# Two layers of state-space mixing and routed experts: the second layer's output with tokens on partitions, its mean from centred matrices, D x seeded by ScalarE, the gate by tanh

## The chip, the core and the metric

The kernel runs on one core of a Trainium2 chip. A core has TensorE (PE; its weight loads are listed as PEld), VectorE (DVE), ScalarE (ACT), GpSimd (POOL) and SyncE (SP, which here only issues DMAs), a memory SBUF and an accumulator memory PSUM, both of 128 partitions. Each engine executes its own queue in order; semaphores tie the queues together. The metric is the device time of one execution in microseconds, the lower the better.

## What is computed

Everything is fp32. The input x is (4, 256, 64, 64), that is 16384 tokens of 256 channels. The reference, cut to what the change touches:

```python
# layer 0, per batch; tokens = x as (L = 4096, 256), times w_in.T
z   = sigmoid(silu(tokens @ w_gate.T + b_gate))
t   = layernorm(tokens)
...                                   # Mamba scan with D_INNER = 512, 16 states
y   = ys + Dp * xm                    # xm: the convolved, Silu'd input of the scan
y   = (y * silu(zm)) @ out_w.T
x1  = tokens + (y * z) @ w_out.T + x  # the residual of layer 0

# layer 1, on t = x1 as tokens
u   = layernorm(t)                    # eps 1e-5
xn  = rmsnorm(u)
...                                   # SSD with 8 heads of 64, 64 states
y   = rmsnorm(y * silu(z), 1e-5)
t   = t + (u + y @ W_out.T)
logits = layernorm(t) @ gate_w + gate_b          # 8 experts, the best one is taken
t   = t + prob * expert(layernorm(t))            # capacity 2560 tokens per expert
```

## The kernel before

Three stages follow each other: `mixers` (both mixing layers and the routing, to about 6035 us of the profiled execution), `experts` (to about 7360 us) and `turn` (the transposition of the result). The change lies in `mixers`, but for the place of some columns in a row that the experts read.

`mixers` works on 64 chunks of T = 256 tokens (16 in each of 4 batches). Channels lie on partitions, tokens along the free dimension. For a chunk the parts are recorded by functions: `front0` (projections, norm and convolution of layer 0), `mid0` (gate, dt, B and C), `scan` (the recurrence, in 16 units of 1024 columns: ACT makes the decays `da`, DVE multiplies `ub` and scans `h`, POOL multiplies `p` with C, PE sums over states into `py`), `tail0` (output of layer 0 and the residual x1), `front1` (norms, projections and convolution of layer 1), `ssd` (two blocks of 128 tokens, s = 0 and 1) and `back1` (output of layer 1, routing).

Nothing is issued while it is recorded. `Plan` keeps every operation with its reads, its writes, an assumed duration (the `weight`s in `mm`, `act`, `dve`, `gps`) and a slot: chunk number times 16 plus the number in `at(...)`. `Plan.order` is a list scheduler over the five queues: at each moment an engine takes, among the operations that could start, the one with the smallest slot. A tile with `bufs` buffers is begun only when one is free, and DVE operations that read two SBUF tensors are kept apart from POOL's. The result is a fixed order on each engine. So a change of one operation or of one weight can move all the others. `silus` keeps the Silus of one point together, between two loads of ACT's tables.

What the change touches, with the names and lines of before:

- `D x`: `scan` puts `diag_d0[:, j]` times `gx` into `py` by a matmul (line 846), before the 16 sums of that j. `py` has one buffer for two j. DVE multiplies it with the gate's half of `gx` into `g`, 256 columns for each j (line 859).
- The gate: `mid0` makes sigmoid of the Silu by Exp, Ln and Exp on ACT (lines 738, 743, 744) and stores it as `z_d`; `tail0` loads it and multiplies (line 874).
- x1 and its norm: `tail0` copies x1 from PSUM (line 883); `front1` makes its mean with the constant matrix `mean_c` (line 892), subtracts it on DVE (`xc`, line 894), squares, averages, makes two reciprocal roots (one for xn, one for u) and the residual `res` = u + x1 by two DVE operations (lines 911, 912).
- The state of `ssd`: decay times state, and the addition of the new part (lines 1064, 1065), each 256 columns, twice a chunk.
- `back1`: the mean of squares over 512 channels by `mean_c` (line 1078), `W_out` as the stationary operand with 256 tokens moving (line 1084), `t2` = product x root + `res` by two DVE operations (lines 1086, 1087), then the transposition of `t2` to tokens on partitions (line 1094), the routing scores as a further product (line 1098), a copy into `row` (line 1103), from which the tokens go out, and the statistics for the experts' norm.

The setup, ahead of `r = Plan(tc)`, is written directly and stands first in every queue.

Of the kernel before, what the change touches and what calls it, by code (L numbers as in the profile page):

```python
# [20 lines left out]
P = 128  # L21
# [24 lines left out]
ROW = C + 4  # L46
# [86 lines left out]
class Plan:  # L133
# [67 lines left out]
    def mm(self, out, left, right, **kw):  # L201
        rows, n = out.shape[0], self.width(right)
        w = max(0.3, n / 600) if rows > 64 else max(0.2, n / 1000) if rows > 32 else max(0.2, n / 1100)
        self.note("PE", w, self.nc.tensor.matmul, (out, left, right), kw, (out,), (left, right), join=out.root)
# [162 lines left out]
def tile_conv_attn_hybrid(ctx: ExitStack, tc: tile.TileContext, a: dict, out: bass.AP, cap: int, st: int):  # L367
# [36 lines left out]
    def mixers(es):  # L404
# [45 lines left out]
        s_out = load("W_out", nc.scalar)  # L450
# [7 lines left out]
        for k in range(KD):  # L458
            ts(s_out[:, k], s_out[:, k], s_gn[:, k : k + 1], None, ALU.mult)
# [17 lines left out]
        before = mask("before", -1, -1, 1)  # L477
# [10 lines left out]
        diag_d0 = diagonal(m_d, "diag_d0")  # L488
# [52 lines left out]

        m_inb = wp.tile([P, 2 * KD], F32, name="m_inb", tag="m_inb")
# [16 lines left out]

        rank = wp.tile([P, NE], F32, name="rank", tag="rank")  # L560
# [11 lines left out]
        nc.gpsimd.memset(blank[:, C + 3 :], float(NT))  # L572
# [35 lines left out]
        def silus(*tiles):  # L608

            calls = [(nc.scalar.activation, (t, t, AF.Silu), t, t) for t in tiles]  # L610
            calls.append((nc.scalar.preload_act_table_set, (SETS,), None, None))
# [50 lines left out]
        class Chunk:  # L662
            def __init__(self, i, b, c):
                self.i, self.b, self.c = i, b, c

            def at(self, n):

                r.slot(self.i * NST, n)
# [55 lines left out]
        def mid0(k_):  # L724
# [5 lines left out]
            r.dma("ACT", k_.gx_d.rearrange("k p l -> p k l"), pre0[:, KC:])  # L730
            k_.at(MID0 + 1)
# [4 lines left out]

            z = pre0[:, :KC]
            r.act(z, z, AF.Exp, scale=-1.0)
# [4 lines left out]
            r.act(z, z, AF.Ln, bias=one_c)  # L743
            r.act(z, z, AF.Exp, scale=-1.0)
            k_.z_d = scratch([KC, P, T], "z_d")
            r.dma("ACT", k_.z_d.rearrange("k p l -> p k l"), z)
# [41 lines left out]
        def scan(k_):  # L788
# [11 lines left out]
            for j in range(KD):  # L800
# [10 lines left out]
                dt4, u4 = both  # L811

                gx = work([P, 2, T], "gx", 2)
                r.dma("SP", gx, k_.gx_d.rearrange("(s j) p l -> j p s l", s=2)[j])
                sl = slice(j * SQ, (j + 1) * SQ)
                if later:

                    k_.at(j * SQ - 1)
# [4 lines left out]
                for f in range(SQ):  # L823
# [19 lines left out]
                    if f == 0:  # L843
                        if j % 2 == 0:
                            py = bank_y(2, T)
                        r.mm(py[:, j % 2], diag_d0[:, j], gx[:, 1], start=True, stop=False, skip_group_check=True)
                    for i in range(SQ):
# [5 lines left out]
                            stop=f == SQ - 1 and i == SQ - 1,  # L853
# [5 lines left out]
                r.tt(k_.g[:, j], gx[:, 0], py[:, j % 2], ALU.mult)  # L859
# [3 lines left out]
        def tail0(k_):  # L863
# [10 lines left out]
            r.tt(z, z, po, ALU.mult)  # L874
# [7 lines left out]
            k_.x1 = x1 = z  # L882
            r.copy(x1, po)

        def front1(k_):

            first = k_.c == 0
            x1 = k_.x1
            k_.at(TAIL + 2)
            pm = bank_b(T)  # L890
            for k in range(KC):
                r.mm(pm, mean_c, x1[:, k], start=k == 0, stop=k == KC - 1)
            xc = work([P, KC, T], "xc1")
            r.tt(xc, x1, pm[:, None, :].to_broadcast([P, KC, T]), ALU.subtract)
# [3 lines left out]
            pv = bank_b(T)  # L898
            for k in range(KC):
                r.mm(pv, mean_c, sq[:, k], start=k == 0, stop=k == KC - 1)  # L900

            rboth = work([P, T], "rstd", 2)
            rstd = work([P, T], "rstd", 2)
            r.act(rboth, pv, AF.Ln, bias=epsb_c, scale=1.0 + EPS)
            r.act(rstd, pv, AF.Ln, bias=eps5_c)
            r.act(rboth, rboth, AF.Exp, scale=-0.5)
            r.act(rstd, rstd, AF.Exp, scale=-0.5)
            xn = work([P, KC, T], "t")
            r.tt(xn, xc, over_channels(rboth), ALU.mult)
            k_.res = res = work([P, KC, T], "res1", 2)  # L910
            r.tt(res, xc, over_channels(rstd), ALU.mult)
            r.tt(res, res, x1, ALU.add)
# [476 lines left out]
```

## Time and profile before

| | us |
|---|---|
| median of 3 runs | 7476.55 |
| lowest and highest of them | 7471.62, 7479.49 |
| the profiled execution | 7447.88 |
| its span, first to last instruction | 7446.1 |
| busy in it: PE, DVE | 6483.4, 5935.5 |
| busy in it: ACT, POOL | 4791.0, 3129.4 |
| mean granted TensorE clock | 0.938 of full speed |

The rows below and the prediction come from the profiled execution. A group of instructions is given by its line in the source, its engine, its operation, the tile written and the tiles read (buffer numbers left out), the shapes and the count; then the busy time, the mean duration of one, and the idle time of the engine just before these instructions, with what ended it. Nearly all operations of `mixers` have the line 356, where the plan issues them, so they are told apart by their tiles. An fp32 matmul stands as two MATMUL and two LDWEIGHTS records. Busy time counts overlapping records once; a mean counts each in full.

### The profile page before, as it was taken

The numbers are of one execution on the slowest core, as the hardware profiler recorded it, in microseconds if no ns is written. First come the engines' busy times: TensorE is split into PE (matmuls) and PEld (weight loads), VectorE is DVE, ScalarE is ACT, GpSimd is POOL, SyncE is SP. The second block draws the span as 40 slices with busy tenths as digits, with TensorE's granted clock in tenths as the row PEclk, the third lists the DMA queues.
The fourth block names the chain that finished last, engine by engine and source line by source line (L and its number), as shares of the span: only waits on it lengthen the run. The fifth ranks groups of instructions, "written<-read, shape, count | busy, mean of one in ns | idle before, by whom it ended". The sixth has DMA issues, their size and how long they took to land. (4 is left out here: it accounts for less than half of the span.)

```text
span 7446.1 us, 114562 instructions
## 1 busy us (share of the span) xinstructions
PE 6483.4 (87%) x38320; PEld 4211.9 (57%) x38320; DVE 5935.5 (80%) x7459; ACT 4791.0 (64%) x11351; POOL 3129.4 (42%) x2436
## 2 busy tenths in 40 slices
PE   4788888888888888888988888888888879999996
PEld 3555555555555555555555555555555556666664
DVE  4799999999999999999999999999999823333332
ACT  4677787777777788777877777777777621111111
POOL 3455455454455455555554555554555401111110
PEclk7899999999999999999999999999999889999998
DMA  7766666666666666666666666666666321111115
GB/s 196 206 171 170 170 172 166 170 170 168 172 169 170 169 169 167 173 174 172 175 172 170 169 170 172 171 170 170 168 174 170 101 63 43 50 45 37 44 32 185
DMA packets 1157215, 1106.25 MB, mean 149 GB/s; under 512 B 127512, under 2 KB 1137316, under 8 KB 1156370
## 3 DMA queue, kind: packets, MB, share of 16 engines
q1 hardware_dynamic: 967362, 884.52, 46.9%
q10 hardware_dynamic: 175440, 180.83, 7.4%
q0 software_dynamic: 13824, 33.58, 1.3%
q8 instruction: 305, 5.00, 0.3%
q14 instruction: 284, 2.33, 0.1%
HBM read 780.64 MB, written 313.85 MB: 147 GB/s over the span
## 5 line engine op out<-in xcount | busy, mean ns | idle before, releaser
L356 POOL TENSOR_TENSOR p<-h,bc 128x1024 f32<-128x1024 f32 x1024 | 2414.9, 2359 | 2133.6 <-DVE ub L356 1221.2
L356 DVE TENSOR_TENSOR_SCAN h<-da,ub 128x1024 f32<-128x1024 f32 x1024 | 2339.7, 2285 | 108.0 <-ACT da L356 6.2
L356 ACT ACTIVATE da<-dt,w_m_Alog 128x255 f32<-128x255 f32 x4096 | 1807.4, 498 | 94.3 <-DMA dt<-dt_d 80.7
L356 DVE TENSOR_TENSOR ub<-u,bc 128x1024 f32<-128x1024 f32 x1024 | 1367.7, 1336 | 34.3 <-DMA u<-u_d 13.9
L356 PE MATMUL py<-p,sum 128*32 128x256 f32 x8192 | 704.4, 420 | 194.4 <-POOL p L356 192.2
L1246 ACT ACTIVATE hid<-ph,b 128x512 f32<-128x512 f32 x160 | 109.2, 682 | 1029.7 <-PE ph L1244 871.4
L1266 POOL DMA_INDIRECT tok_d<-fixed,number x160 | 156.9, 981 | 1164.8 <-DVE fixed L1264 833.0
L356 PE MATMUL b<-t,w_W_in 128*128 128x256 f32 x2304 | 594.9, 401 | 27.7 <-DVE dv L356 18.1
L1255 PE MATMUL po<-w,hid 128*128 128x256 f32 x2560 | 591.2, 384 | 5.1 <-DVE y L1257 5.0
L1244 PE MATMUL ph<-xt,w 128*128 128x512 f32 x1280 | 561.7, 597 | 14.1 <-DVE xt L1239 14.1
L1255 PEld LDWEIGHTS po<-w,hid 128*128 128x128 f32 x2560 | 476.7, 190 | 122.3 <-issue 55.6
L356 PEld LDWEIGHTS b<-t,w_W_in 128*128 128x128 f32 x2304 | 429.0, 195 | 150.4 <-DVE dv L356 45.9
L356 PEld LDWEIGHTS py<-p,sum 128*32 128x32 f32 x8192 | 200.7, 114 | 537.3 <-POOL p L356 314.2
L356 PE MATMUL a<-t,w_m_in_w 128*128 128x256 f32 x2048 | 479.9, 388 | 10.9 <-DVE t L356 10.7
L356 PEld LDWEIGHTS a<-t,w_m_in_w 128*128 128x128 f32 x2048 | 381.3, 191 | 113.1 <-DVE t L356 26.0
L356 ACT COPY hlast<-h 128x4 f32<-128x4 f32 x1024 | 197.0, 196 | 381.5 <-DVE h L356 358.5
L1244 PEld LDWEIGHTS ph<-xt,w 128*128 128x128 f32 x1280 | 240.6, 190 | 311.8 <-issue 287.5
L1257 DVE TENSOR_SCALAR y<-po,rows 128x256 f32<-128x256 f32 x160 | 76.4, 481 | 380.0 <-PE po L1256 380.0
L356 ACT ACTIVATE pre<-pre 128x512 f32<-128x512 f32 (+2 forms) x256 | 352.5, 1377 | 12.8 <-ACT dbl L356 9.7
L356 PE MATMUL c<-cum,after 128*128 128x512 f32 x512 | 330.0, 762 | 32.5 <-DVE state L356 27.9
L356 PE MATMUL b<-raw,taps_x 128*32 128x256 f32 x2048 | 175.0, 414 | 206.4 <-DMA raw<-raw_d 150.2
L356 ACT ACTIVATE cum<-upto,da 128x128 f32<-128x128 f32 x1024 | 333.9, 391 | 4.8 <-DVE da L356 4.5
(224 smaller groups left out, 11461.6 us busy)
## 6 DMA issues: line engine op xcount, KB each, us to landing
raw<-raw_d SPq DMA_DIRECT2D x2048, 128.0 KB
dt<-dt_d SPq DMA_DIRECT2D x1024, 128.0 KB
u<-u_d SPq DMA_DIRECT2D x1024, 128.0 KB
raw_d<-raw ACTq DMA_DIRECT2D x128, 518.0 KB
gx_d<-pre ACTq DMA_DIRECT2D x64, 1024.0 KB
gx<-gx_d SPq DMA_DIRECT2D x256, 256.0 KB
bc<-bc_d SPq DMA_DIRECT2D x2048, 32.0 KB
dt_d<-mid SPq DMA_DIRECT2D x64, 512.0 KB
```

Source lines behind the costliest of these rows:

```text
L356: op.issued = f(*map(placed, args), **{k: placed(v) for k, v in kw.items()})
L1244: mm(ph, w1[:, k, f * P : (f + 1) * P], xt[:, k], start=k == 0, stop=k == KC - 1)
L1246: act(hid[:, f], ph, AF.Relu, bias=b1[:, f : f + 1])
L1255: mm(po, hid[:, f, j * P : (j + 1) * P], w2[:, f], start=f == 0, stop=False)
L1257: ts(y[:, j], po, rows[:, j, C : C + 1], None, ALU.mult)
L1266: nc.gpsimd.indirect_dma_start(out=tok_d, out_offset=bass.IndirectOffsetOnAxis(ap=number[:, j : j + 1], axis=0), in_=fixed[:, j], in_offse ...
```

## The change

- The matrices of layer 0's residual (`w_in` plus the identity) and output (`w_out`, halved) have their mean over output channels taken out in the setup, so that what `tail0` copies from PSUM is already the centred x1, `xc`. The mean itself is made only as a column per token, from the vectors `mean_res` and `mean_out`.
- `front1` makes the reciprocal root of the norm twice: as before over all partitions for xn, and as a column per token (`cols`) together with the mean. Each column comes from matmuls with the tokens as the stationary operand and one moving column. `res` is gone.
- `back1` transposes `xc` and adds the score columns in the same bank; ACT scales it with `cols` into `xr`, that is the residual u + x1 and its scores, tokens on partitions. `W_out` has eight more columns (its product with the scores' matrix, made in the setup) and is now the moving operand, the tokens the stationary one. One DVE operation per 128 tokens makes product x root + `xr` straight into `row`. The statistics and the scores read `row`.
- `D x`: ACT writes it into `py` as a scaled copy, for two j at once, ahead of the sums; `g` is made for two j, 512 columns, and `gx` loaded for two.
- The gate: sigmoid(v) is (1 + tanh(v/2))/2. The Tanh stands with the Silus, the 1 is added in the multiplication of `tail0`, the half is in `w_out`.
- The state: one scalar_tensor_tensor for each of four 64-column heads, in place of two instructions over all.
- The plan's weight of a matmul with at most 16 columns is 0.13 instead of 0.3. The four routing columns of `row` stand ahead of the 256 channels instead of behind.

```diff
     def mm(self, out, left, right, **kw):
-        w = max(0.3, n / 600) if rows > 64 else max(0.2, n / 1000) if rows > 32 else max(0.2, n / 1100)
+        w = 0.13 if n <= 16 else max(0.3, n / 600) if rows > 64 else max(0.2, n / 1000) if rows > 32 else max(0.2, n / 1100)
...
-        diag_d0 = diagonal(m_d, "diag_d0")
...
+        def centre(w, name):
+            means = wp.tile([P, KC], F32, name=name, tag=name)
+            for k in range(KC):
+                nc.vector.tensor_reduce(means[:, k : k + 1], w[:, k], AX.X, ALU.add)
+            ts(means, means, 1.0 / C, None, ALU.mult)
+            for k in range(KC):
+                ts(w[:, k], w[:, k], means[:, k : k + 1], None, ALU.subtract)
+            return means
+
+        mean_res = centre(w_res, "mean_res")
+        ts(w_out, w_out, 0.5, None, ALU.mult)
+        mean_out = centre(w_out, "mean_out")
...
+        for k in range(KD):
+            pt_s = bank_a()
+            for m in range(KC):
+                nc.tensor.transpose(pt_s[:, m * P : (m + 1) * P], s_out[:, k, m * P : (m + 1) * P], ident)
+            turned = wk.tile([P, KC, P], F32, name=nm("turned"), tag="sq", bufs=1)
+            nc.scalar.copy(turned, pt_s[:, :C].rearrange("p (m l) -> p m l", m=KC))
+            pt_s = bank_a()
+            for m in range(KC):
+                mm(pt_s[:, :NE], turned[:, m], g_cen[:, m], start=m == 0, stop=m == KC - 1)
+            nc.scalar.copy(s_out[:, k, C:], pt_s[:, :NE])
+
+        py = py_p.tile([P, 512], F32, name="py0", tag="py", bufs=1)
+        mm(py, ident, s_in[:, 0, :512], start=True, stop=True)
...
+        def half_tanh(t):
+            return nc.scalar.activation(t, t, AF.Tanh, scale=0.5)
+
-        def silus(*tiles):
+        def silus(*tiles, gates=0):
             calls = [(nc.scalar.activation, (t, t, AF.Silu), t, t) for t in tiles]
+            calls += [(half_tanh, (t[:, :KC],), t[:, :KC], t[:, :KC]) for t in tiles[:gates]]
...
-            r.act(z, z, AF.Exp, scale=-1.0)
-            r.act(z, z, AF.Ln, bias=one_c)
-            r.act(z, z, AF.Exp, scale=-1.0)
...
-                gx = work([P, 2, T], "gx", 2)
-                r.dma("SP", gx, k_.gx_d.rearrange("(s j) p l -> j p s l", s=2)[j])
+                if j % 2 == 0:
+                    gx = work([P, 2, 2, T], "gx", 2)
+                    for s in range(2):
+                        r.dma("SP", gx[:, s], k_.gx_d[s * KD + j : s * KD + j + 2].rearrange("j p l -> p j l"))
...
-                        r.mm(py[:, j % 2], diag_d0[:, j], gx[:, 1], start=True, stop=False, skip_group_check=True)
+                            for i in range(2):
+                                r.act(py[:, i], gx[:, 1, i], AF.Copy, scale=m_d[:, j + i : j + i + 1])
...
-                r.tt(k_.g[:, j], gx[:, 0], py[:, j % 2], ALU.mult)
+                if j % 2 == 1:
+                    r.tt(k_.g[:, j - 1 : j + 1], gx[:, 0], py, ALU.mult)
...
-            r.tt(z, z, po, ALU.mult)
+            r.dve("scalar_tensor_tensor", z, z, 1.0, po, ALU.add, ALU.mult)
...
-            k_.x1 = x1 = z
-            r.copy(x1, po)
+            k_.xc = work([P, KC, T], "xc", 2)
+            r.copy(k_.xc, po)
+            k_.x1 = (xin, z)
...
-            pm = bank_b(T)
-            for k in range(KC):
-                r.mm(pm, mean_c, x1[:, k], start=k == 0, stop=k == KC - 1)
-            xc = work([P, KC, T], "xc1")
-            r.tt(xc, x1, pm[:, None, :].to_broadcast([P, KC, T]), ALU.subtract)
...
+            for s in range(NS):
+                for k in range(KC):
+                    r.mm(pv[:, T + s : T + s + 1], sq[:, k, s * Q : (s + 1) * Q], mean_c[:, :1], ...)
+            for s in range(NS):
+                for i, (part, means) in enumerate(zip(k_.x1, (mean_res, mean_out))):
+                    for k in range(KC):
+                        r.mm(pv[:, T + NS + s : T + NS + s + 1], part[:, k, s * Q : (s + 1) * Q], means[:, k : k + 1], ...)
...
-            r.act(rstd, pv, AF.Ln, bias=eps5_c)
+            r.act(cols[:, :NS], pv[:, T : T + NS], AF.Ln, bias=eps5_c)
+            r.copy(cols[:, NS:], pv[:, T + NS :])
...
-            r.tt(res, xc, over_channels(rstd), ALU.mult)
-            r.tt(res, res, x1, ALU.add)
+            r.act(cols[:, :NS], cols[:, :NS], AF.Exp, scale=-0.5)
+            r.act(cols[:, :NS], cols[:, :NS], AF.Identity, bias=one_c)
...
-                r.tt(new, state, hend[:, :, None].to_broadcast([P, hh, HD]), ALU.mult)
-                r.tt(new, new, ph, ALU.add)
+                for h in range(hh):
+                    r.dve("scalar_tensor_tensor", new[:, h], state[:, h], hend[:, h : h + 1], ph[:, h], ALU.mult, ALU.add)
...
+            for s in range(NS):
+                pr = bank_c(C + NE)
+                for k in range(KC):
+                    r.transpose(pr[:, k * P : (k + 1) * P], k_.xc[:, k, toks], ident)
+                for k in range(KC):
+                    r.mm(pr[:, C:], k_.xc[:, k, toks], g_cen[:, k], start=k == 0, stop=k == KC - 1)
+                xr = work([P, C + NE], "xr", 2)
+                r.act(xr, pr, AF.Identity, scale=k_.cols[:, s : s + 1], bias=k_.cols[:, NS + s : NS + s + 1])
...
-            for k in range(KD):
-                r.mm(pm, mean_c, k_.sq[:, k], start=k == 0, stop=k == KD - 1)
+            for s in range(NS):
+                for k in range(KD):
+                    r.mm(pm[:, s : s + 1], k_.sq[:, k, s * Q : (s + 1) * Q], mean_c[:, :1], ...)
...
-            r.tt(t2, po, over_channels(rr), ALU.mult)
-            r.tt(t2, t2, k_.res, ALU.add)
+                for k in range(KD):
+                    r.mm(po, sz[:, k, s * Q : (s + 1) * Q], s_out[:, k], start=k == 0, stop=k == KD - 1)
+                r.dve("scalar_tensor_tensor", row[:, s, TOK:], po, rr[:, s : s + 1], xrs[s], ALU.mult, ALU.add)
...
-            for s in range(NS):
-                r.copy(row[:, s, :C], pr[:, s])
```

## The prediction

> **What bounds the kernel now.** I read the page's slices first, then the busy time of each engine by stage, then the groups of instructions inside a steady millisecond of the first stage, then the waits there, and last the timeline of the setup.
>
> The slices (tenths of busy time in 40 equal parts of the span) show two regimes: 32 slices in which VectorE (DVE) is at nine tenths, then eight in which TensorE (PE) is.
>
> ```profile
> PE   4788888888888888888988888888888879999996
> DVE  4799999999999999999999999999999823333332
> ACT  4677787777777788777877777777777621111111
> ```
>
> Busy time by stage, in the column order of the first line:
>
> ```profile
> core 0: us, PE busy (x) PEld busy (x) DVE busy (x) ACT busy (x) POOL busy (x), PEclk, DMA share, GB/s
> 2500.00:3500.00 1000.00, 877.28 (x5776) 573.20 (x5775) 930.68 (x1153) 789.96 (x1890) 507.38 (x380) 0.95 0.66 171
> 6100.00:7200.00 1100.00, 1083.11 (x3797) 675.64 (x3795) 415.70 (x577) 160.06 (x272) 133.36 (x136) 1.00 0.14 42
> ```
>
> The second is the experts, PE-bound, and the change leaves their arithmetic alone. The first is the stage it edits. DVE has 69 us of idle time in 1000. The groups of that millisecond (busy us, mean ns of one, then the idle time just before them):
>
> ```profile
> L356 DVE TENSOR_TENSOR_SCAN h<-da,ub 128x1024 f32<-128x1024 f32 x177 | 404.4, 2285 | 17.4 <-DVE ub L356 0.7
> ...
> L356 DVE TENSOR_TENSOR g<-gx,py 128x256 f32<-128x256 f32 x44 | 18.1, 411 | 17.4 <-PE py L356 17.1
> L356 DVE SCALAR_TENSOR_TENSOR mid<-mid,mid 128x1024 f32<-128x1024 f32 x11 | 16.1, 1461 | 8.2 <-ACT mid L356 8.1
> L356 DVE TENSOR_TENSOR state<-state,dend 128x256 f32<-128x256 f32 x22 | 15.9, 722 | 0.0
> ...
> L356 DVE TENSOR_TENSOR state<-state,c 128x256 f32<-128x256 f32 x22 | 8.9, 407 | 0.3
> ...
> L356 DVE TENSOR_TENSOR res<-res,z 128x512 f32<-128x512 f32 x11 | 7.6, 692 | 0.4
> L356 DVE TENSOR_TENSOR t<-t,res 128x512 f32<-128x512 f32 x11 | 7.6, 692 | 0.4
> ...
> L356 DVE TENSOR_TENSOR gm<-c,upto 128x128 f32<-128x128 f32 x22 | 6.0, 271 | 2.7 <-PE c L356 2.7
> ```
>
> 177 scans are 11.06 chunks of 16, so a chunk takes 90.4 us: DVE works 84.1 of it and idles 6.3, PE 79.3, ScalarE (ACT) 71.4, POOL 45.9. The idle time lies in many small waits, the largest named one 17.1 us for g on PE (1.5 per chunk). DVE sets the pace; PE is the next, 11 us behind.
>
> **VectorE, per chunk.** Gone: the centring xc<-z,b 0.678, the two of res 0.685 and 0.692, t<-c,rstd 0.670 and t<-t,res 0.692, in all 3.42. Replaced: z 0.676, four g at 0.411 (1.64), and twice the pair of state instructions, 2 x (0.722 + 0.407) = 2.26. Together 8.00 us.
>
> New: z as scalar_tensor_tensor of 512, not in the trace; the same shape as tensor_tensor is 0.676, half of the 1024-wide scalar_tensor_tensor row is 0.73, the row's excess over its tensor_tensor twin (1.461 - 1.217) added whole gives 0.92; I take 0.70. Two g of 512 at 0.68: 1.36. Eight state instructions of 64 columns: scalar_tensor_tensor of 16 columns took 0.17 to 0.19, gm with 128 columns 0.27; a per-partition pointer may add the 0.07 by which the experts' TENSOR_SCALAR y<-po,rows (0.481) exceeds a tensor_tensor of 256 (0.411). Ends 0.17 and 0.29, I take 0.23: 1.84. Two of row (264 columns from PSUM): ends 0.41 and 0.49, I take 0.45: 0.90. The statistics read SBUF in place of PSUM at the same 0.43. New in all 4.80 (ends 4.2 and 5.6), so DVE loses 3.2 us (2.4 to 3.8): 80.9.
>
> **TensorE, per chunk.** These are the groups that go, and the nearest to what comes:
>
> ```profile
> L356 PE MATMUL c<-cum,mean_c 128*128 128x256 f32 x88 | 20.8, 379 | 0.0
> ...
> L356 PE MATMUL py<-gx,diag_d 128*128 128x256 f32 x88 | 29.3, 415 | 5.0 <-DVE g L356 4.5
> ...
> L356 PE MATMUL b<-z,mean_c 128*128 128x256 f32 x44 | 12.9, 418 | 0.0
> L356 PE MATMUL b<-w_W_in,t 128*128 128x8 f32 x88 | 11.6, 259 | 3.5 <-ACT rbc L356 3.5
> ```
>
> Each fp32 matmul is two records. Gone: 2.65 (D x), 1.17 (mean of x1), 1.88 (mean of squares), 5.70 in all. New: 20 matmuls with one output column. The setup has that very form, 16 of them as 32 records:
>
> ```profile
> 23.73 4.05 PE L546 MATMUL bank_a<-w_ln_b,w_m_in_w 128*128 128x1 f32 x32
> ```
>
> That is 0.25 each, as the 8-column row gives too (11.6 us over 44 matmuls is 0.26): these cost their weights, not their column. 20 x 0.25 = 5.0, and W_out with 264 columns instead of 256 adds 8/256 of 3.60, 0.11. PE loses 0.6. The ends: 0.19 each (one LDWEIGHTS record) gives -1.8, 0.38 (two that do not overlap) +2.0. I take the setup's row, being the same form.
>
> "TensorE: Matmul & The Clock Gate", section "Back-to-back issue gap", has about 60 cycles, some 25 ns, as the isolated gap of a matmul of 1 to 64 columns. By it 20 matmuls of two records would be an estimated 1.0 us and PE would lose 4.6; the setup's row is five times that and decides.
>
> **ScalarE, per chunk.** Gone: the gate's Exp, Ln, Exp (2 x 0.629 + 0.722 = 1.98), Ln and two Exp of 256 columns in front1 and back1 of the rstd kind (0.462 + 2 x 0.414 + 0.469 = 1.76), two row copies (0.74): 4.48. New: Tanh of 512 at the Exp row's 0.629; six instructions of 2 to 4 columns at 0.2 to 0.3, 1.52; two xr of 264 with two pointers, the form of the experts' tn<-rows (12 in 6.00 us, so 0.50): 1.02; four seeds py<-gx with a pointer, priced as da of 255 columns, 0.498: 2.0. In all 5.2, so +0.7, 72.1. The z copy turns into the xc copy at the same price. The change adds no ACT_TABLE_LOAD: the built programs have 258 each; one more per chunk would be 1.28 us of ACT.
>
> "ScalarE: Activation LUTs", "Rules for kernel authors", would keep multiplications off ScalarE, VectorE being faster per element; that speaks against the seeds and xr. By the rule the four seeds alone, as tensor_tensor of 0.411, would put 1.64 us back on DVE and halve the gain; the trace has ACT at 79% and DVE at 93%, so occupancy decides for the move here.
>
> **Queues.** SP issues the same number of transfers per chunk: gx as two 256 KB transfers every second j in place of one per j. ACT still issues z_d, now beside gx_d and without the three instructions ahead. POOL's p, scatters and adds stay. Nothing new stands behind a DMA wait, so I cost this at nothing; its cover is the prefetch of AHEAD = 4 units, 22 us, and without it a late gx would show as a wait of ACT's seeds. What changes in kind: ACT now waits in order for g before it seeds py, and PE's sums wait for ACT. Behind the seeds on ACT are the decays da of later units, and DVE's scans wait for these, but da has three buffers.
>
> **Setup and tail.** Setup adds, ahead of the first matmul of the stage, DVE's centring (some ten short instructions, 0.17 to 0.37 each, 3 us) and four rounds of transposes, copy, product with the scores' matrix, copy: each 0.5 + 0.37 + 0.5 with three handovers of 0.1, 1.65; the last copy is off the path. With one 512-wide matmul the stage's first matmul moves from 28.5 to some 38.5 us: +10 once (5 to 14). The drain of the last chunk loses the mean matmuls, the centring, one of two additions, the transposes and a row copy and gains the short matmuls: some -3.
>
> **Sum.** Per chunk DVE has 80.9 us of work. Its idle time, 6.3 now, I let grow to 6.8, because PE goes from 88 to 90% of the period and in-order waits on it lengthen; half of the g waits go. 87.7 against 90.4: -2.7, times 64 is -173; with +10 and -3, -166. The profiled execution took 7447.9 us (span 7446.1), 0.4% under the median of the runs, 7476.6, and under the lowest, 7471.6; I carry the difference over: profile 7282, median 7311.
>
> **Rivals.**
> 1. PE becomes the bound. For: it is at 88%, and the 20 short matmuls may cost 0.38. Against: the setup's row, and 98% busy in the experts shows that PE can run dense. PE at 81.3 and 7 to 8 us of its present 11 of waits gives 88.3 to 89.3, -1.1 to -2.1 per chunk: 7350 to 7413.
> 2. Slower: the seeds. py has one buffer. Today PE re-fills it itself after g (0.6 us); now DVE's g, ACT's two seeds (1.0) and PE's sums stand in series, twice a chunk, and ACT's block of table load, Silu of 2560 columns, Tanh, table load lasts 1.28 + 2.34 + 0.63 + 1.28 = 5.5 us. If seeds fall behind it, p's two buffers fill, then h's three, and DVE stops. It decides from 3.2 us per chunk of new DVE idle, 1.6 per handover; one whole block per chunk would be +2.3 x 64 + 7: 7630. Against: a unit lasts 5.6 us, and ACT's order in the changed program puts the seeds ahead of the Silu block.
> 3. No change: the chain from chunk to chunk, not DVE's sum, sets the period, and the freed time becomes waits (6.3 to 9.5 idle): 7477 to 7490. Against: no single wait of DVE is over 1.6 us per chunk.
>
> **How the numbers follow.** Forecast 0.58 (own range 7240 to 7400: DVE's -3.8 with idle unchanged, and -2.4 with idle up by 1.1), PE bound 0.18, no change 0.05, slower 0.19. What a measurement can tell from no change is 0.2%, 15 us. Faster 0.76, same 0.05, slower 0.19. The range, 7235 to 7500, leaves out most of rival 2 and a little below.
>
> **What would show it.** Right: per chunk 80 to 82 us of DVE work, state rows near 0.23, 128x1 matmuls near 0.25, period 87 to 88.5, first steady matmul ten us later. Wrong: a wait of PE on ACT for py of over 1 us per handover, or DVE's idle above 9 us per chunk, or state rows near 0.3.

## The result, and the profile after

The changed kernel takes 7889.6 us (median of 4 runs, 7879.7 to 7895.1), the kernel before on the same chip 7475.2: ratio 1.0553, 95% interval 1.0534 to 1.0571. It is 414 us slower; forecast were 7311, and at most 7500. Below, "before" and "after" are the two kernels, e1 to e18 the experiments.

The slices of the page of the changed kernel: the first regime now has VectorE at eight tenths where it had nine, and the granted clock changes between eight and nine.

```profile
PE   5788888888888888888888888888888879999997
DVE  3788888888888888888888888888888843333332
ACT  3677777777777777777777777777677731111111
PEclk7788888988988888998898889888889879999998
```

The granted clock of before, on its page:

```profile
PEclk7899999999999999999999999999999889999998
```

Busy time by stage of the changed kernel, columns as in the prediction (us and records of PE, weight loads, VectorE, ScalarE, POOL, then the granted clock): a steady millisecond, 5000 us of the first stage, and half a millisecond of the experts.

```profile
2500.00:3500.00 1000.00, 868.40 (x5631) 587.36 (x5630) 856.96 (x1067) 733.03 (x1804) 487.31 (x350) 0.89 0.62 159
500.00:5500.00 5000.00, 4316.67 (x27809) 2888.61 (x27801) 4262.24 (x5314) 3661.31 (x8981) 2445.94 (x1768) 0.89 0.62 158
6500.00:7000.00 500.00, 493.41 (x1737) 309.22 (x1736) 185.78 (x259) 71.31 (x121) 58.83 (x60) 1.00 0.14 42
```

The experts run as before at full clock; the loss lies in the first stage. Its 5000 us hold 818 scans, 51.1 chunks of 16; those of before hold 880, 55.0 chunks, with this row:

```profile
500.00:5500.00 5000.00, 4377.57 (x28817) 2868.08 (x28816) 4654.21 (x5783) 3933.93 (x9447) 2532.65 (x1903) 0.95 0.65 170
```

| per chunk, us | before | after |
|---|---|---|
| period | 90.9 | 97.8 |
| VectorE busy | 84.6 | 83.4 |
| VectorE idle | 6.3 | 14.4 |
| PE busy | 79.6 | 84.4 |
| granted clock | 0.95 | 0.89 |

6.9 us times 64 chunks is 442, and the spans of the two profiled executions differ by 443 (7889.4 against 7446.1); the medians differ by 414, since the profiled execution of before was 27 us under its median. VectorE did lose work, but its idle time more than doubled, and PE, forecast to lose 0.6 us, gained 4.8. The groups of the steady millisecond of the changed kernel (busy us, mean ns | idle before):

```profile
L359 DVE SCALAR_TENSOR_TENSOR row<-c,rr,xr 128x264 f32<-128x264 f32 x22 | 10.8, 489 | 53.2 <-PE c L359 31.1 <-ACT e L359 17.2 <-issue 4.8
...
L359 DVE SCALAR_TENSOR_TENSOR z<-z,b 128x512 f32<-128x512 f32 x10 | 6.8, 683 | 13.5 <-PE b L359 13.5
...
L359 PE MATMUL c<-w_W_out,pre 128*128 128x264 f32 x176 | 64.0, 540 | 0.0
L359 PE MATMUL c<-mean_c,cum 128*128 128x1 f32 x176 | 36.2, 336 | 0.0
```

VectorE stands 53.2 us (eleven chunks' worth, 4.8 each) before `row`, the operation that takes the output product from PSUM. The view puts 17.2 of them down to ScalarE's `e`, but over the 5000 us every `row` that waited started within 0.25 us of the end of a record of that product. The product takes 540 ns a record at 264 columns, where it took 379 at 256 in before:

```profile
L356 PE MATMUL c<-pre,w_W_out 128*128 128x256 f32 x176 | 39.8, 379 | 0.0
```

The timeline of PE in after shows where this comes from (start, duration, instructions run together):

```profile
2898.33 1.11 PE L359 MATMUL b<-sq,mean_c 128*128 128x256 f32 x4
2899.27 0.95 PE L359 MATMUL b<-mean_c,sq 128*128 128x1 f32 x8
2900.08 0.58 PE L359 MATMUL b<-mean_res,xtail 128*128 128x1 f32 x4
...
2901.42 0.58 PE L359 MATMUL b<-mean_out,z 128*128 128x1 f32 x4
...
2903.13 2.68 PE L359 MATMUL c<-mean_c,cum 128*128 128x1 f32 x16
2905.67 6.42 PE L359 MATMUL c<-w_W_out,pre 128*128 128x264 f32 x16
```

and the busy time of the stretches around it:

```profile
2896.00:2904.00 8.00, 8.00 (x71) 6.32 (x69) 7.16 (x10) 7.12 (x14) 2.36 (x1) 1.00 0.20 56
2904.00:2911.00 7.00, 7.00 (x22) 5.86 (x22) 3.10 (x5) 5.00 (x16) 2.57 (x2) 0.51 0.23 72
2911.00:2925.00 14.00, 13.38 (x81) 10.39 (x79) 13.55 (x23) 6.93 (x21) 6.97 (x6) 1.00 0.77 246
```

PE was busy for all of the 8 us before (the profile models where a matmul ends, so this says that PE had work in hand, not how much of it was used). From about 2904 on, 1 us after the first of `back1`'s eight short ones started, the clock is halved for some 7 us, the output product takes 6.42 us, and VectorE has 3.10 us of work in 7. In before the same product is one run of 3.62 us:

```profile
2525.23 3.62 PE L356 MATMUL c<-pre,w_W_out 128*128 128x256 f32 x16
```

So the theory: the matmuls with one column, twelve of `front1` and eight of `back1` in 7 us, are mostly weight loads and let the granted clock fall though PE is busy; the dense product that follows runs at half speed, and VectorE waits in order for it. The rivals: the order that the plan made (its weight of 0.13 against some 0.25 measured), the seeds on ScalarE, or the other parts.

### The profile page after: what moved, and what is told of

It reads as the page before. It is cut to its first block, busy times and chain, and to the rows that moved or that the text cites. A ratio compares the mean times of both kernels' runs of the same rounds, so it can differ in the third digit from the quotient of the medians.

```text
span 7889.4 us, 117156 instructions
## 1 busy us (share of the span) xinstructions
PE 6807.6 (86%) x39626; PEld 4504.7 (57%) x39626; DVE 5861.7 (74%) x7406; ACT 4803.5 (61%) x11615; POOL 3227.1 (41%) x2431
## 5 line engine op out<-in xcount | busy, mean ns | idle before, releaser
L359 ACT ACTIVATE da<-dt,w_m_Alog 128x255 f32<-128x255 f32 x4096 | 1805.4, 498 | 14.8 <-DMA dt<-dt_d 13.3
L359 DVE TENSOR_TENSOR ub<-u,bc 128x1024 f32<-128x1024 f32 x1024 | 1443.2, 1409 | 44.0 <-DMA u<-u_d 13.9
L359 PE MATMUL py<-p,sum 128*32 128x256 f32 x8192 | 728.6, 440 | 200.1 <-POOL p L359 196.9
L1299 PE MATMUL ph<-xt,w 128*128 128x512 f32 x1280 | 562.4, 597 | 14.1 <-DVE xt L1294 14.1
L359 PEld LDWEIGHTS py<-p,sum 128*32 128x32 f32 x8192 | 224.4, 119 | 535.1 <-POOL p L359 298.0
L359 PEld LDWEIGHTS b<-t,w_W_in 128*128 128x128 f32 x2304 | 437.1, 196 | 127.5 <-DVE hot L359 18.5
L359 PE MATMUL a<-t,w_m_in_w 128*128 128x256 f32 x2048 | 499.5, 393 | 6.8 <-DVE t L359 6.8
L359 PE MATMUL a<-raw,taps_m 128*32 128x256 f32 x2048 | 192.3, 451 | 289.1 <-DMA raw<-raw_d 250.1
L359 PE MATMUL c<-cum,after 128*128 128x512 f32 x512 | 372.9, 828 | 24.7 <-DVE state L359 23.0
L359 PE MATMUL c<-w_W_out,pre 128*128 128x264 f32 x1024 | 384.7, 554 | 0.0
```

The lines of the kernel that those rows point to most:

```text
L359: op.issued = f(*map(placed, args), **{k: placed(v) for k, v in kw.items()})
L1299: mm(ph, w1[:, k, f * P : (f + 1) * P], xt[:, k], start=k == 0, stop=k == KC - 1)
```

## The experiments

All ratios are to the kernel before, which took 7475 to 7481 in these jobs. The clock is that of 500 to 5500 us.

| run | edit | us | ratio, 95% | clock |
|---|---|---|---|---|
| after | | 7889.6 | 1.0553 [1.0534, 1.0571] | 0.89 |
| e1_wide | after, 20 short matmuls widened | 7587.9 | 1.0140 [1.0121, 1.0159] | 0.93 |
| e8_wide_pm | after, only `back1`'s eight widened | 7742.3 | 1.0353 [1.0325, 1.0380] | 0.90 |
| e9_wide_all | e1, the 8-column ones too | 7596.1 | 1.0153 [1.0132, 1.0174] | 0.92 |
| e2_weight | after, plan weight 0.3 | 7786.4 | 1.0401 [1.0382, 1.0419] | 0.88 |
| e5_wide_w25 | e1, plan weight 0.25 | 7758.9 | 1.0366 [1.0341, 1.0392] | 0.91 |
| e6_wide_w30 | e1, plan weight 0.3 | 7623.1 | 1.0186 [1.0167, 1.0206] | 0.94 |
| e3_peseed | after, D x by PE | 8019.2 | 1.0724 [1.0703, 1.0744] | 0.88 |
| e14_wide_peseed | e1, D x by PE | 7728.6 | 1.0337 [1.0317, 1.0356] | 0.92 |
| e4_before_short | before, mean of squares by short matmuls | 7575.7 | 1.0123 [1.0106, 1.0140] | 0.93 |
| e7_before_seeds | before, D x by ScalarE | 7519.8 | 1.0056 [1.0037, 1.0074] | 0.91 |
| e15_before_gate | before, gate by Tanh | 7631.3 | 1.0203 [1.0183, 1.0223] | 0.92 |
| e16_before_state | before, state by one operation a head | 7508.9 | 1.0042 [1.0030, 1.0054] | 0.94 |
| e10_before_wide | before, its 8-column matmuls widened | 7464.0 | 0.9980 [0.9971, 0.9989] | 0.95 |
| e11_before_w13 | before, plan weight 0.13 to 16 columns | 7418.0 | 0.9923 [0.9906, 0.9940] | 0.94 |
| e12_before_w25 | the same with 0.25 | 7496.6 | 1.0020 [1.0011, 1.0030] | 0.93 |
| e13_before_w13_wide | e10 and e11 | 7428.5 | 0.9932 [0.9916, 0.9948] | 0.94 |
| e17_wide_noraw | e1, convolutions without their loads | 7707.1 | 1.0311 [1.0294, 1.0328] | 0.92 |
| e18_before_noraw | before, the same | 7810.6 | 1.0452 [1.0435, 1.0470] | 0.91 |

### Only the width of the short matmuls

```diff
-  r.mm(pm[:, s : s + 1], k_.sq[:, k, ...], mean_c[:, :1], ...)
+  r.mm(pm[:, s * 128 : (s + 1) * 128], k_.sq[:, k, ...], mean_c[:, :128], weight=0.13, ...)
-  r.mm(pv[:, T + s : T + s + 1], sq[:, k, ...], mean_c[:, :1], ...)
+  r.mm(pv[:, T + s * 64 : T + (s + 1) * 64], sq[:, k, ...], mean_c[:, :64], weight=0.13, ...)
   (mean_res and mean_out likewise, their column broadcast to 64)
```

The weights loaded, the plan's order on every queue and the numbers stay; only the matrix is streamed through by 64 or 128 equal columns instead of one.

> The changed kernel with its 20 one-column matmuls per chunk made wide, 128 columns for the mean of squares in back1 and 64 in front1 (equal columns, one is read); the plan's weight for them stays 0.13, so the order on all five queues is that of the changed kernel. Clock theory (matmuls that only load weights count as an idle array, the granted clock is halved, and the product with W_out behind them runs at half speed): granted clock back from 0.89 to 0.93 or more in the steady stage, W_out product from 0.73 us per matmul to 0.46 to 0.50, VectorE's wait before row from 5 us per chunk to under 2, time 7400 to 7650. Plan theory (weight 0.13 is too small, VectorE stands in order at row for a PE that the plan had done): the order is unchanged, so the wait at row stays over 4 us per chunk and the time within 100 us of 7890. Seed theory (ACT's seeds of py hold PE and POOL): no change, 7850 to 7930.

7587.9, 302 us less than after, 4.5 us per chunk (857 scans in 5000 us, a period of 93.3). The groups of its steady millisecond:

```profile
L359 PE MATMUL c<-w_W_out,pre 128*128 128x264 f32 x176 | 41.0, 387 | 0.0
L359 PE MATMUL c<-mean_c,cum 128*128 128x128 f32 x176 | 22.4, 281 | 0.0
...
L359 DVE SCALAR_TENSOR_TENSOR row<-c,rr,xr 128x264 f32<-128x264 f32 x22 | 10.6, 481 | 8.3 <-ACT mid L359 4.3 <-PE c L359 3.9
...
L359 DVE SCALAR_TENSOR_TENSOR z<-z,b 128x512 f32<-128x512 f32 x10 | 6.9, 687 | 19.1 <-PE b L359 19.1
```

The same 176 records with 128 columns took less time than with one (22.4 us against 36.2), the product is back at 387 ns, and the idle time before `row` falls from 53.2 to 8.3 us, 4.1 of the 4.5 us per chunk. That one-column matmuls lower the granted clock, and that this is 302 of the 414 us, is shown. What sets the clock is not: that it goes by columns streamed, not by occupancy, is a reading that fits, no more.

```diff
 e8:  only the eight of back1 as above
 e9:  as e1, and
-  r.mm(pr[:, C:], k_.xc[:, k, toks], g_cen[:, k], ...)
+  r.mm(pr[:, C:], k_.xc[:, k, toks], g_cen[:, k, None].to_broadcast([P, 16, NE]), weight=0.13, ...)
   (the dt projection likewise, with 128 columns of the matrix around its eight)
```

> The changed kernel with the eight matmuls of back1 alone made wide (128 columns), the twelve of front1 left at one column; order as in the changed kernel. If the group directly ahead of the product with W_out sets its clock: most of the 300 us comes back, 7590 to 7700. If the gate answers to the front1 group some microseconds earlier in PE's order: W_out stays above 0.6 us per matmul and the time at 7780 to 7890. If both fill the same window: between, 7700 to 7780.

> The first run (20 one-column matmuls made 64 and 128 wide) with the eight 8-column matmuls of a chunk (dt of layer 1, scores on xc) made 128 wide as well, their moving operand repeated or taken wider; order that of the changed kernel on all queues. Clock theory: these too only load weights and make low windows, so the granted clock rises from 0.926 to 0.935 or more and the time falls by 30 to 90 us from 7588: 7500 to 7560. If the rest of the loss is the order of the queues and not the clock: 7570 to 7600.

Widening `back1`'s eight brings 147 us of the 302: both groups count, the twelve of `front1` for the rest. In that run the product is nearly back at its speed, but the eight wide ones take 388 ns instead of 281 (groups of its steady millisecond):

```profile
L359 PE MATMUL c<-w_W_out,pre 128*128 128x264 f32 x160 | 38.5, 395 | 0.0
L359 PE MATMUL c<-mean_c,cum 128*128 128x128 f32 x160 | 32.7, 388 | 0.0
```

They now stand in the half-speed stretch that `front1`'s short ones leave, so these twelve, with 8-column matmuls and transposes among them, are enough to halve the clock for a while. Widening the 8-column matmuls as well brings nothing (+8 us, the intervals overlap), so there one short group fewer is not better.

### The short matmuls alone, in the kernel before

```diff
-  for k in range(KD): r.mm(pm, mean_c, k_.sq[:, k], ...)          # 256 columns
+  for s in range(NS):
+      for k in range(KD): r.mm(pm[:, s : s + 1], k_.sq[:, k, ...], mean_c[:, :1], ...)
```

> The kernel before with one part alone: the mean of squares in back1 by eight one-column matmuls with the tokens stationary instead of four of 256 columns; ACT then takes the root of a broadcast column, so that the same number of columns is written (two Ln of 128 instead of one of 256; the numbers are not the reference's, since tokens then lie on partitions while the product has them on the free dimension). The plan's weight for them is the old 0.3. Clock theory: the W_out product behind them slows from 0.45 to 0.55 to 0.7 us per matmul, the clock falls from 0.945 to 0.91 to 0.93, time 7520 to 7700. Plan theory: the weight is enough for 0.25, so 7450 to 7510.

+97 us, but the product after them was not slowed, as the groups of its steady millisecond show,

```profile
L356 PE MATMUL c<-pre,w_W_out 128*128 128x256 f32 x160 | 37.0, 384 | 0.0
...
L356 PE MATMUL c<-mean_c,cum 128*128 128x1 f32 x160 | 18.4, 245 | 0.0
...
L356 DVE TENSOR_TENSOR g<-gx,py 128x256 f32<-128x256 f32 x43 | 17.7, 412 | 32.0 <-PE py L356 32.0
```

and the eight cost 0.23 us each (18.4 us over 80), close to the 0.25 of the prediction. Eight short matmuls among dense ones did not halve the clock right behind them; in after twenty come within 7 us. So the time lies in the range that the clock theory gave, but not by the mechanism that it gave. The clock of the stage still fell to 0.93, and `g` waits 32.0 us for PE where it waited 17.1; how much of that is the new order is not separated.

### The plan's weight

```diff
 e2, of after:  -  w = 0.13 if n <= 16 else max(0.3, n / 600) ...
                +  w = max(0.3, n / 600) ...
 e5, e6, of e1: 0.25 and 0.3 in place of 0.13, for the widened ones too
 e11, e12, of before: +  w = 0.13 (0.25) if n <= 16 else max(0.3, n / 600) ...
```

> The changed kernel with the plan's old weight rule (0.3 for a matmul of few columns), the matmuls themselves unchanged. Plan theory: the plan now sees 0.3 for what takes 0.25, puts row later, the wait before row falls under 2 us per chunk, time 7400 to 7650. Clock theory: one-column matmuls still stand in groups, the clock stays at 0.88 to 0.90, W_out stays above 0.6 us per matmul; the wait may move from VectorE to elsewhere, time 7700 to 7950. Seed theory: no change.

> The wide matmuls of the first run and, on top, the plan's weight of every matmul of at most 16 columns and of the wide ones at 0.25, near what they take, instead of 0.13. If clock and weight are two separate losses, they add up: 300 us from the width and some 100 from the weight, 7430 to 7530, VectorE idle at z, g, row and gm together under 3 us per chunk. If the weight only mattered because the clock made the matmuls slow, the time stays at 7560 to 7620.

> As the run with 0.25, with the weight of before, 0.3, a little over what they take. Two separate losses: within 40 us of the run with 0.25. If the order that comes out by chance matters more than the weight itself: more than 60 us away from it, on either side.

> The kernel before with one part of the change alone: the plan's weight of matmuls with at most 16 columns 0.13 instead of 0.3 (13 such matmuls per chunk, layer 1's dt, scores, decays and positions); every instruction stays, only their order may change. If the order by itself is worth tens of microseconds: 7500 to 7600, or 7380 to 7450. If the weight harms only because it underrates 20 more matmuls: 7465 to 7495.

> The same with 0.25, what these matmuls take. If the weight's truth matters: equal to before or better, 7430 to 7480. If the order is a matter of chance: on either side of the run with 0.13, and more than 30 us from 7478.

These edits change no instruction, only the order. With the short matmuls 0.3 is 103 us better than 0.13, with the wide ones 35 worse, and 0.25, nearest to what was measured, 171 worse; in before 0.13 is some 60 us better than 0.3 (0.77%), and 0.25 some 16 worse (0.2%). So a truer weight is not a better one, and the order alone moves this kernel by tens of us up to 170. In the steady millisecond of e2 the product is as slow as in after, but VectorE stands less before `row`:

```profile
L359 PE MATMUL c<-w_W_out,pre 128*128 128x264 f32 x160 | 58.3, 542 | 0.0
...
L359 DVE SCALAR_TENSOR_TENSOR row<-c,rr,xr 128x264 f32<-128x264 f32 x20 | 9.6, 486 | 13.8 <-issue 7.0 <-ACT da L359 4.9 <-PE c L359 1.7
```

So the order settles where the half-speed product makes VectorE wait. It does not remove the wait: VectorE's idle time is 13.1 us per chunk in e2 (680.1 of the 5000 over 51.8 chunks) against 14.4 in after, and the scans now wait 103.1 us of the 5000 for POOL's `p`.

### The seeds

```diff
 e3, e14, of after and e1:
-  r.act(py[:, i], gx[:, 1, i], AF.Copy, scale=m_d[:, j + i : j + i + 1])
+  r.mm(py[:, j % 2], diag_d1[:, j], gx[:, 1, j % 2], start=True, stop=False, ...)
 e7, of before:
-  r.mm(py[:, j % 2], diag_d0[:, j], gx[:, 1], start=True, stop=False, ...)
+  r.act(py[:, j % 2], gx[:, 1], AF.Copy, scale=m_d[:, j : j + 1])
```

(In e3 and e14 the diagonal matrix is that of layer 1's D; both D are all ones in the inputs, so the values stay.)

> The changed kernel with D x put into py by PE again, one matmul of 256 columns per j with the diagonal matrix (that of layer 1's D is used for layer 0 as well, both being all ones in the inputs), g still made for two j. Seed theory: the chain g, ACT, PE was the loss, time 7300 to 7500. Clock theory: four dense matmuls per chunk more on PE raise the clock by at most 0.01 and cost 2 us of PE, time 7800 to 7950. Plan theory: 7800 to 7950.

> The changed kernel with wide matmuls (128 in back1, 64 in front1) and D x put into py by PE again (with layer 1's diagonal matrix, both D being all ones). Seed theory for what is left of the loss (110 us over before in the first run): 7480 to 7560. If the seeds relieve PE on balance: four more dense matmuls, 7600 to 7720. If only the density of PE's work counts: clock up from 0.926 by 0.005 to 0.015 at the same time, 7560 to 7610.

> The kernel before with one part alone: ACT writes D x into py as a scaled copy, for each j by itself, in place of PE's matmul with the diagonal matrix; g stays one instruction per j. By the prediction's sum PE is relieved of 2.65 us per chunk, ACT takes 2.0: PE comes earlier, VectorE's waits shrink by 0.3 to 1.5 us per chunk, 7380 to 7460. Seed theory (g, ACT and PE in series over one buffer): VectorE's idle rises, 7500 to 7650. Clock theory: four dense matmuls fewer per chunk lower PE's activity, the granted clock falls by 0.01 to 0.02, which takes part of the relief back: 7430 to 7500.

Undone, the seeds cost 130 and 141 us, alone in before they cost 41. Each of these edits also gives a new order, the same one in e3 and e14, and the order is worth as much; so with the rest of the change the seeds seem to help, but that is not shown apart from the order. In e7 PE sheds D x, but its clock falls to 0.91, and its busy time stays 79.6 us per chunk (4318.6 us over 868 scans, 54.25 chunks). VectorE's wait for `g` goes, and waits for `gm` and the decays come (its waits in the steady millisecond: us in total, times, longest):

```profile
DVE gm L356 <- PE c L356: 29.0, 11, 3.4
DVE h L356 <- ACT da L356: 23.7, 10, 3.3
```

### Gate and state alone, and the widths of before

```diff
 e15: the three operations of the sigmoid out, half_tanh in silus, 1 added in tail0's multiplication, w_out halved
 e16:
-  r.tt(new, state, hend..., ALU.mult)
-  r.tt(new, new, ph, ALU.add)
+  for h in range(hh): r.dve("scalar_tensor_tensor", new[:, h], state[:, h], hend[:, h : h + 1], ph[:, h], ...)
 e10, e13: before's own 8-column matmuls 128 wide, as in e9; e13 with the weight of e11
```

> The kernel before with one part alone: the gate by Tanh beside the Silu, w_out halved, the 1 added in the multiplication of tail0. ACT loses 1.35 us per chunk and the chain to the decays of the next chunk two instructions. By the prediction's sum nothing on VectorE or PE changes: 7440 to 7480. As a cause of the loss: over 7510. By chance of the order alone it may be 60 us off on either side, as the weight runs were.

> The kernel before with one part alone: the state by eight scalar_tensor_tensor of 64 columns in place of four instructions of 256. In the changed kernel each takes 0.274, 2.2 us per chunk against 2.26: nothing gained in VectorE's work, and its first half no longer runs ahead of PE's product, so it waits 0.6 us per chunk more: 7480 to 7530. If the waits of the port for POOL (0.5 us per chunk in the old form) go for good: 7440 to 7475.

> The kernel before with its own eight 8-column matmuls per chunk made 128 wide in the same way; order that of the kernel before on all queues. Clock theory: granted clock up by up to 0.005, 7440 to 7475, which would be faster than both kernels. If these few make no low window: 7470 to 7490.

> The kernel before with the plan's weight 0.13 for matmuls of at most 16 columns, and its eight 8-column matmuls 128 wide; order that of the weight run. Both edits gained alone (7418 and 7464 against 7480). Clock theory or not, if they add up: 7395 to 7410, the fastest so far. If the width is worth nothing in this order: 7413 to 7425.

Each part alone makes before slower: gate +156, state +34 (each against 7475), seeds +41, short mean +97. Together 328, while after, which has all of them and more, is 414 above before; without the short mean 231, while e1, where it is wide, is 109 above. The parts do not add, and each also changes the order, which is worth as much. Why the gate alone costs 156 stays open. Widening before's 8-column matmuls, order kept, brings 0.2% (the interval excludes 1 narrowly); on top of e11 it brings nothing.

e11 at 7418.0 beats both kernels, by 0.77% and by 6%; it is the kernel before with one weight of the plan changed.

### What is left: late loads

TensorE's waits in 5000 us of after (us in total, times, longest):

```profile
PE b L359 <- DMA raw<-raw_d: 199.8, 49, 5.2
PE a L359 <- DMA raw<-raw_d: 177.2, 86, 6.0
```

377 us, 7.4 per chunk, for the tokens of the two convolutions; before 176.2, 3.2 per chunk; e1 391.6, 7.3. On SyncE's queue, which issues these loads, a wait has grown from 11.2 us in before:

```profile
SPq L359 <- PE b L359: 339.1, 94, 8.9
```

Half of these waits (51 of 94) stand at the loads into `xtail`, which the short matmuls of `front1` now read. That could have been the 109 us left. With the loads made, but the matmuls not waiting for them:

```diff
-  r.mm(pi[...], weights[:, j * SQ + i], raw4[:, i], ...)
+  (planned as reading raw4, issued with m_in[:, 0, :T] in its place)
```

> The kernel after with wide columns (the first experiment), same order on every queue, but the two convolutions' matmuls take a constant matrix as their moving operand instead of the tokens loaded for them (the loads are still made, the numbers of both layers are not the reference's). So TensorE no longer waits for these loads. In the trace of the first experiment TensorE waits 392 us of 5000 for them, 7.3 us per chunk; in before 176 us, 3.2 per chunk; in after 377, 7.4. Theory A (what is left between the first experiment and before, 109 us, is TensorE standing in order behind late loads): this kernel falls by at least 100 us more than the kernel before does under the same edit, and the two end within 30 us of each other. Theory B (the waits for the loads are slack that another wait takes over, or the rest is the clock and the dearer parts): both fall alike, within 40 us, and the gap stays 70 to 150 us.

> The kernel before with the same edit: the two convolutions' matmuls take a constant matrix instead of the loaded tokens, the loads are still made, same order on every queue; the numbers are not the reference's. Both theories: a fall of at most 3.2 us per chunk, 200 us, since TensorE waits 176 us of 5000 for these loads; likelier 0 to 100, VectorE being the bound here. Theory A: this and the run above end within 30 us. Theory B: 70 to 150 us apart.

Both theories failed: both kernels became slower, e17 by 119 us and e18 by 335, with every queue in its old order. In e18 TensorE's idle time moved to waits for POOL's products (in before 127.5 us of 5000, now 363.9), POOL stood for `dt` (waits of e18 in the same 5000 us):

```profile
POOL e L356 <- DMA dt<-dt_d: 484.6, 96, 12.2
```

(101.5 before), and the clock fell to 0.91. Why `dt` came later stays open. The edit takes out more than TensorE's wait: the loads no longer wait for these matmuls either (SyncE's waits for `b` are 63 in e17, 103 in e1). So the two runs show that taking the wait away does not gain its time, not what it was worth. What makes the 109 us between before and e1 stays open; order, clock (0.93) and the waits for late loads all differ, and no run took one alone.

## Why the prediction was wrong

**VectorE, right in kind, mis-sized.** Forecast -3.2 us per chunk. By the rows of after: z 0.683 (taken 0.70), g 0.680, state 0.274 (0.23, so 2.19 instead of 1.84), row 0.489 (0.45): 5.2 come in place of 8.0, -2.8. State is near the 0.3 named as a sign of error. Of the 2.8, 1.7 us came back: `ub` took 1416 ns in place of 1335 over the 5000 us (16 a chunk, 1.3 us), the scalar_tensor_tensor of `mid` 1771 in place of 1405 (0.4). 84.6 - 2.8 + 1.7 is 83.5; measured 83.4. That agrees in part by luck: other rows moved as well, two operations into `cdec` and one into `hot` by -0.7 together. e1 has `ub` and `mid` at 1399 and 1880, so the clock is not their reason; which work they met stays open.

**TensorE: the step that failed.** "20 x 0.25 = 5.0", "PE loses 0.6". The price is right at full clock (0.24 for the four of `front1`'s squares, 10.4 us over 44; 0.23 in e4), and the setup's row was a better guide than the 25 ns of the Trainium skill ("TensorE: Matmul & The Clock Gate", "Back-to-back issue gap"), of which the page itself says that it leaves out the weight loads. What failed is that the sum took the clock of before, 0.95, as given, so that the short matmuls cost nothing beyond their own time. In after `back1`'s eight, mostly at half clock, cost 0.41 each (36.2 us over 88), and the output product 5.8 us a chunk (64.0 over 11) instead of 3.71; these two make 3.4 of the 5.4 us between PE's forecast -0.6 and its measured +4.8. `front1`'s other eight stand at 0.30 by busy time, but pairs of them start 0.45 us apart at full clock in the timeline above, so they are not dearer than priced.

The sign of it stood in the trace of before, right behind the row that the prediction took as its price. The clock is halved there as well, with PE busy throughout, and the first product of the stage takes 3.76 us, which takes 2.00 in the steady stage (two windows with the columns as above, then the timeline of PE):

```profile
27.00:28.40 1.40, 1.40 (x8) 1.40 (x8) 1.01 (x2) 0.57 (x2) 1.40 (x4) 0.50 0.00 0
28.40:32.20 3.80, 3.80 (x11) 3.08 (x11) 0.61 (x3) 0.88 (x1) 3.80 (x11) 0.50 0.01 2
...
28.49 3.76 PE L356 MATMUL a<-xin,w_cen 128*128 128x256 f32 x8
...
2519.61 2.00 PE L356 MATMUL a<-xin,w_cen 128*128 128x256 f32 x8
```

This step is 302 us of the miss. With the short ones wide, in e1, PE is busy 80.4 us a chunk, but VectorE works 83.2 and idles 10.2 (forecast 80.9 and 6.8), and the time is still 277 us over the forecast. What makes VectorE's idle time there stays open.

The same page of the Trainium skill, "TensorE: Matmul & The Clock Gate", gives in "Part 1: The HAM clock gate" the gate two states, half and full clock, set by how busy PE has been recently, in windows of some 3.4 us; the trace agrees with the two values (0.51 and 1.00 in neighbouring stretches). Its rule in "HAM oscillation — how this bites in real kernels" is against idle gaps of PE over some 3.4 us; here PE was busy 8.00 of 8.00 us ahead of the halved stretch, so the measurement goes further than the rule. "Part 4: PE-mode transpose" says that transposes do not count as busy in the same way; no run here separates the transposes, but the one-column matmuls of after look like that.

**VectorE's idle time.** "6.3 now, I let grow to 6.8": it was 14.4, over the 9 that the prediction named as a sign of being wrong. The largest new wait, `row`, is an in-order wait that the prediction didn't list: in before VectorE did not wait at the operation that took the product (`t<-c,rstd`, 0.0 us). e1 takes it nearly away; what remains of idle time there, 10.2, is spread over waits for PE (z 19.1 us of 1000, was 1.1).

**Queues.** "Nothing new stands behind a DMA wait, so I cost this at nothing." SyncE's queue got the wait on TensorE shown above, and the loads of the convolutions came later. What that costs is not settled by the two runs.

**The plan's order.** The sum had no term for it. The weight alone moves the kernel by up to 171 us, as much as the gain forecast.

**Setup.** Forecast +10 (5 to 14): the first matmul of the stage stands at 42.62 us, before at 28.49, so +14.1, just over the range. Of the 4 us too many, 2.8 lie in the setup's own one-column matmuls, the same 32 records that took 4.05 us in before. The timeline of after:

```profile
24.98 6.83 PE L561 MATMUL bank_a<-w_ln_b,w_m_in_w 128*128 128x1 f32 x32
...
42.62 2.47 PE L359 MATMUL a<-xin,w_cen 128*128 128x256 f32 x8
```

**The rivals.** The first had PE dearer by short matmuls at 0.38, and had 7413 at most; the average in after is 0.33 by busy time (36.2, 13.3, 13.1 and 10.4 us over 220), but it left out that dense work slows too. The second, seeds in series, did not happen: ScalarE waited 2.4 us of 1000 for `g`, a seed took 0.470 (priced 0.498), `g` waits 6.5 us for PE where it waited 17.1, and undoing the seeds, in a new order, costs 130 us. The third, freed time turning into waits, is nearest in kind, but it had the idle time at 9.5.

## What to carry to other kernels

Before replacing wide matmuls by one-column ones, look at what runs right after them: a group of some twenty, mostly weight loads, halved the clock for a stretch of some 7 us here, and widening them, at hardly any cost in TensorE's time, took 302 us back. Where the order comes from a planner, a change of costs is a change of order: compare it at a kept order first, and expect weights alone to be worth a per cent or two either way. And follow the clock behind a row that is taken as a price: the slow product behind it was in the trace of before. A wait seen in the trace is not yet a cost; the two runs that removed one became slower.

## What was unexpected of the hardware

- The granted clock was halved while PE was busy without a gap in the profile (8.00 of 8.00 us ahead, 7.00 of 7.00 at 0.51), during 20 one-column matmuls; with the same weights and 64 or 128 columns the stage's clock rose from 0.89 to 0.93.
- A matmul of 128 columns costs hardly more than one of a single column: 0.25 us (22.4 us over 88) against 0.23 to 0.24 at full clock.
- An instruction mix with fewer matmuls need not free TensorE: without D x, and in the new order that this gave, its busy time per chunk was unchanged at 79.6 us, at a clock of 0.91 instead of 0.95.
